# Two index conversions moved behind the last output projection's sums

## The chip, the cores and the metric

The kernel runs on one core of one Trainium2 chip. The metric is device time in microseconds (us) of one execution. An execution that was also recorded by the hardware profiler gives the trace; its times count from the first instruction, and the time from first to last instruction is the span.

## The reference, cut to what matters

One layer over 8 sequences of 1024 tokens with 512 features, all in float32:

```python
xn = _layernorm(x)
s = rnn(xn)                  # three projections 512 -> 1024 (W1), gates, a scan over time, then @ W2 (1024 -> 512)
f = (silu(xn @ sg) * (xn @ su)) @ sd          # shared feed-forward
f += routed(xn)              # each token to the one of 32 experts with the highest logit:
                             #   xs = xn * sigmoid(top logit);  (silu(xs @ gw[e]) * (xs @ uw[e])) @ dw[e]
x = x + s * silu(f)
```

## The kernel before, in words

The work has two stages with a short passage between them.

**Stage one** walks over 16 chunks of 512 tokens. For each chunk it computes the W1 projections, the scan and the shared feed-forward's hidden values, and projects the previous chunk's results out through W2 and the shared down matrix. All products of this stage use a seven-product scheme for 2x2 blocks, so operands are sums and differences of blocks. The order of all instructions is written out by hand: `at(slot, step)` puts a step into a numbered slot, a loop counts `now` up and runs the steps of each slot, and `due(now)` says how many matmuls of the output projection (`fill`, the generator `project_out`) must have been issued by then. Each engine carries out its instructions in the order in which they were issued.

One output projection is one `unit`: a chunk and a half (half 0 is W2, half 1 the shared down matrix). There are 32 units (n = 0 to 31). A unit has seven products of 16 matmul records each (8 matmuls of 128x128 by 128x256, each recorded twice), in the order `UNIT` = P1, P2, P6, P5, P7, P3, P4. P1, P6, P7 and P4 add up in one PSUM tile called `chain`; P2, P5 and P3 in one called `side`. The steps of a unit that matter here:

- L1007 (`out_combine`) makes the left operands: `s1` and `s3` on POOL (GpSimd), `s2` and `s4` on DVE (VectorE). P5 uses s1, P6 s2, P7 s3 and P3 s4.
- L1044 (ACT, ScalarE) copies P1's sum to SBUF (`a1`), later P6's (`a2`, same buffer) and P5's (`b5`).
- L1067 (DVE) adds P2's sum, read from `side`, and `a1` into the result tile `o[0]`. P5 starts `side` afresh, so it must come after L1067. L1067 itself writes a tile that the unit before has stored with L1028, so it must come after that store has landed.
- L1078 (DVE) adds P3's sum and `a2`; L1073 and L1081 (ACT) and L1074 (POOL) finish `o[1]`; L1028 (SP, SyncE) stores the results into `rec2`.
- L985 and L988 (`out_fetch`, SP) load a product's right operand, 512 KB, into a buffer of the pool `wo` or, for the last two units, `far`.

**The passage** builds the routing table. Each token gets a slot with its expert. The table has 186 columns of 128 rows. L1327 writes it to DRAM; L1330 (`ids`, DVE) makes an integer copy `idx`, by which whole rows are gathered: the first expert's inputs (L206, three gathers on POOL) and, later, what an expert needs at its end (L223). Experts 1 to 31 gather their inputs in quarter rows (L213), and need a second table, `fours`: index times 4 plus the quarter's number. `numbers(half)` makes one half of it. It issues four loads of the DRAM table from POOL (L1337) into a tile `number`, and puts one conversion (L1338, DVE, 128x372) into a later slot. Both halves are issued in one slot.

Around it stand, in the order of issue: the last unit (n = 31, half 1), the first expert's transposes on PE (L240) with their copies on DVE (L243), and the loads of the first expert's weights `e_wg`, `e_wu` and `e_wd` (L193, SP, 2 MB each). After it come four memsets of the experts' accumulators (L1489, DVE).

**Stage two** goes through 32 experts. For each, PE does eight rounds of gate, up and down products (L272, L261); ACT and DVE do the SiLU (L277, L279, L280); loads and gathers for the next two experts are issued between the rounds (L193, L213, L223), the next expert's inputs are transposed on DVE from round 5 on (L248), and results are scattered to the output (L360).

Of the kernel before, what the change touches and what calls it, by code (L numbers as in the profile page):

```python
# [33 lines left out]
def tile_kernel(  # L34
# [45 lines left out]
    nc = tc.nc  # L80
# [344 lines left out]
    now = 0  # L425
    steps = {}

    def at(slot, what, *args):
        assert slot >= now
        steps.setdefault(slot, []).append(lambda: what(*args))  # L430
# [655 lines left out]
    class Dispatch:  # L1086
# [245 lines left out]
        def numbers(self, half):  # L1332

            f = self.big([P, 2, NCOL], f"number{half}")
            rows = self.table.rearrange("(b c) q -> c b q", c=BL)[:, 2 * half : 2 * half + 2, :]
            for a in range(NA):
                nc.gpsimd.dma_start(out=f[a * BL : (a + 1) * BL, :, :], in_=rows)  # L1337
            at(now + 3, lambda: nc.vector.tensor_scalar(  # L1338
                pools["fours"][:, 2 * half : 2 * half + 2, :], f, float(NA), piece[:, 0:1],
                ALU.mult, ALU.add,  # L1340
            ))
# [247 lines left out]
```

## Time and profile before

| | |
|---|---|
| median of 3 runs | 4239.5 us (4238.96 to 4239.67) |
| the profiled execution: time | 4237.99 us |
| the profiled execution: span | 4236.3 us |
| PE (TensorE) busy | 4198.9 us, 99% of the span |
| DVE busy | 2083.9 us, 49% |
| ACT busy | 1978.0 us, 47% |
| POOL busy | 1105.3 us, 26% |
| granted TensorE clock, mean over the span | 0.997 of full speed |
| DMA | 925.61 MB, mean 218 GB/s |

PEld is PE's weight load, which runs beside its matmuls. In a timeline, each line gives the start, the duration, the engine and line of the kernel, the operation with output <- inputs and a count; the brackets give how long the engine stood idle ahead of it and what ended that. Entries with "q" (SPq, POOLq) are the engine's own queue of instructions, such as the issue of a transfer. "issue" as a releaser means that the profile shows no event that ended the wait. A transfer's landing is read from the completion events of its semaphore: every one of the 16 DMA engines reports its part.

### The profile page before, as it was taken

The page shows a single profiled execution, that of the slowest core. Times are in us where ns is not written, and L with a number is a line of the kernel's source. Part 1 is how long each engine was busy: PE and PEld are TensorE (multiplying, and loading weights), DVE is VectorE, ACT ScalarE, POOL GpSimd, SP SyncE. Part 2 cuts the span into 40 slices and gives each one's busy share as a digit, 9 for nine tenths or more (in the row PEclk, how much of TensorE's full clock was granted, in tenths as well). Part 3 has the DMA queues.
Part 4 walks back from the last instruction along what each step waited for, and adds up shares of the span by engine and source line. Part 5 has one row for each costly group of instructions (what it writes and reads, how often), then busy time and mean ns, then how long its engine had stood idle before and what let it go on. Part 6 is the DMA issues. An engine that isn't in the chain of part 4 may idle for free.

```text
span 4236.3 us, 51931 instructions
## 1 busy us (share of the span) xinstructions
PE 4198.9 (99%) x18719; PEld 3527.2 (83%) x18719; DVE 2083.9 (49%) x3425; ACT 1978.0 (47%) x3577; POOL 1105.3 (26%) x1182
## 2 busy tenths in 40 slices
PE   9999999999999999999999999999999999999998
PEld 4688888888888888888888888866777788889998
DVE  5555555544554545555545456424444444544444
ACT  5676676666666766666767666501111111111110
POOL 3222122111221121212211225442232333323221
PEclk9999999999999999999999999999999999999999
DMA  8767666666676666766666656575666567677773
GB/s 277 244 214 231 207 216 216 210 223 206 213 226 216 217 213 203 231 202 216 222 210 220 214 177 205 179 267 181 211 227 226 205 236 242 222 253 242 243 263 113
DMA packets 506854, 925.61 MB, mean 218 GB/s; under 512 B 38397, under 2 KB 324509, under 8 KB 498402
## 3 DMA queue, kind: packets, MB, share of 16 engines
q1 hardware_dynamic: 478754, 831.89, 59.2%
q0 software_dynamic: 27840, 90.36, 6.4%
q8 instruction: 150, 2.46, 0.2%
q14 instruction: 110, 0.90, 0.1%
HBM read 805.27 MB, written 134.92 MB: 222 GB/s over the span
## 4 chain that ended last, share of the span: by engine, by line
PE 97%; DVE 1%; DMA 1%; issue 0%; ACT 0%; POOL 0%; SPq 0%; POOLq 0%; ACTq 0%
PE b L759 24%; PE u L1055 18%; PE c L759 12%; PE e_u L272 11%; PE e_g L272 11%; PE acc L261 11%; PE a L759 6%; PE b L710 3%; PE lgp L520 0%; DMA e_xs<-rec,idx 0%; PE lgt L530 0%; PE b L725 0%; DMA x<-in_L_attn_x_dram 0%; DMA e_rest<-rec,idx 0%; POOL s L1007 0%
## 5 line engine op out<-in xcount | busy, mean ns | idle before, releaser
L759 PE MATMUL b<-t,sums 128*128 128x256 f32 x2400 | 616.1, 379 | 1.2 <-DVE t L681 1.2
L1055 PE MATMUL u<-wP,s 128*128 128x256 f32 x2032 | 598.4, 380 | 6.1 <-issue 6.1
L277 ACT ACTIVATE e_sig<-e_g 128x280 f32<-128x280 f32 (+15 forms) x256 | 101.8, 398 | 931.8 <-PE e_g L272 931.6
L272 PE MATMUL e_u<-e_xsT,e_wu 128*128 128x296 f32 (+15 forms) x2048 | 518.0, 396 | 0.0
L272 PE MATMUL e_g<-e_xsT,e_wg 128*128 128x296 f32 (+15 forms) x2048 | 518.0, 396 | 0.0
L261 PE MATMUL acc<-e_h,e_wd 128*128 128x296 f32 (+15 forms) x2048 | 512.8, 396 | 0.0
L759 PEld LDWEIGHTS b<-t,sums 128*128 128x128 f32 x2400 | 454.8, 190 | 63.0 <-ACT a L773 1.3
L272 PEld LDWEIGHTS e_g<-e_xsT,e_wg 128*128 128x128 f32 x2048 | 389.1, 190 | 87.2
L272 PEld LDWEIGHTS e_u<-e_xsT,e_wu 128*128 128x128 f32 x2048 | 389.1, 190 | 87.1
L261 PEld LDWEIGHTS acc<-e_h,e_wd 128*128 128x128 f32 x2048 | 389.1, 190 | 87.1
L1055 PEld LDWEIGHTS u<-wP,s 128*128 128x128 f32 x2032 | 387.2, 191 | 61.1 <-issue 8.3
L279 DVE TENSOR_TENSOR e_sig<-e_sig,e_g 128x280 f32<-128x280 f32 (+15 forms) x256 | 113.1, 442 | 481.6 <-ACT e_sig L277 481.2
L213 POOL DMA_INDIRECT e_xs<-rec,fours x276 | 262.4, 951 | 178.2 <-DMA e_rest<-rec,idx 86.0
L759 PE MATMUL c<-xnT,sums 128*128 128x256 f32 x1200 | 308.0, 379 | 0.0
L759 PE MATMUL c<-t,sums 128*128 128x256 f32 x1200 | 308.0, 379 | 0.0
L759 PE MATMUL b<-xnT,nat 128*128 128x256 f32 x1200 | 308.0, 379 | 0.0
L759 PE MATMUL a<-xnT,nat 128*128 128x256 f32 x1200 | 308.0, 379 | 0.0
L759 PE MATMUL b<-t,nat 128*128 128x256 f32 x1200 | 308.0, 379 | 0.0
L360 POOL DMA_INDIRECT out_dram<-e_rest,idx x84 | 93.1, 1109 | 801.2 <-DVE e_rest L359 798.2
L759 PEld LDWEIGHTS b<-xnT,nat 128*128 128x128 f32 x1200 | 228.0, 190 | 31.4 <-issue 0.5
L759 PEld LDWEIGHTS a<-xnT,nat 128*128 128x128 f32 x1200 | 228.0, 190 | 31.0
L759 PEld LDWEIGHTS c<-t,sums 128*128 128x128 f32 x1200 | 228.0, 190 | 31.0
(243 smaller groups left out, 6381.2 us busy)
## 6 DMA issues: line engine op xcount, KB each, us to landing
sums<-sdram SPq DMA_DIRECT2D x300, 512.0 KB, 4.6
nat<-in_L_attn_W_dram SPq DMA_DIRECT2D x192, 512.0 KB, 4.6
e_wg<-L_ffn_routed_gate_w_dram SPq DMA_DIRECT2D x32, 2048.0 KB, 8.4
e_wu<-n_L_ffn_routed_up_w_dram SPq DMA_DIRECT2D x32, 2048.0 KB, 12.7
e_wd<-L_ffn_routed_down_w_dram SPq DMA_DIRECT2D x32, 2048.0 KB, 19.0
wP<-tdram SPq DMA_DIRECT2D x127, 512.0 KB, 3.5
nat<-L_ffn_shared_gate_w_dram SPq DMA_DIRECT2D x64, 512.0 KB, 4.9
nat<-n_L_ffn_shared_up_w_dram SPq DMA_DIRECT2D x64, 512.0 KB, 4.3
```

The source lines that it names most:

```text
L213: nc.gpsimd.indirect_dma_start(out=r[:, b, :], out_offset=None, in_=rec1.rearrange("n (a d) -> (n a) d", a=NA), in_offset=bass.IndirectOff ...
L261: nc.tensor.matmul(accs[m][:, :W], lhsT=wd[:, j, m * P : (m + 1) * P], rhs=h[:, :W], start=(j == 0), stop=(j == NI - 1),)
L272: nc.tensor.matmul(o[:, :W], lhsT=w[:, k, j * P : (j + 1) * P], rhs=xsT[:, k, :W], start=(k == 0), stop=(k == KH - 1),)
L277: nc.scalar.activation(sig[:, :W], g[:, :W], AF.Sigmoid)
L279: nc.vector.tensor_tensor(sig[:, :W], sig[:, :W], g[:, :W], ALU.mult)
L360: store = nc.gpsimd.indirect_dma_start(out=of[:, :], out_offset=bass.IndirectOffsetOnAxis(ap=col[:n, :], axis=0), in_=o, in_offset=None, b ...
L710: nc.tensor.matmul(ps[:, part], lhsT=natural[n][:, k, block * P : (block + 1) * P], rhs=xnTs[0][:, k, part], start=(k == 0), stop=(k == KH ...
L759: nc.tensor.matmul(ps, lhsT=lhs[:, k, :], rhs=rhs[:, k, :], start=(new and k == 0), stop=(k == KQ - 1),  skip_group_check=True,)
L1055: nc.tensor.matmul(ps[:, q, :], lhsT=lhs[:, q * P : (q + 1) * P], rhs=w[:, p, :],  start=(q == 0 and p == 0 and name in ("P1", "P2", "P5") ...
```

## The change

The slot of the two conversions moves from 3 behind the issue of their loads to 26 behind. Nothing else is edited.

```diff
             for a in range(NA):
                 nc.gpsimd.dma_start(out=f[a * BL : (a + 1) * BL, :, :], in_=rows)
-            at(now + 3, lambda: nc.vector.tensor_scalar(
+            at(now + 26, lambda: nc.vector.tensor_scalar(
                 pools["fours"][:, 2 * half : 2 * half + 2, :], f, float(NA), piece[:, 0:1],
                 ALU.mult, ALU.add,
             ))
```

In the built program only DVE's order differs; the other four engines have the same instructions in the same order. On DVE, from the last part of s2 on:

| before | after |
|---|---|
| L1007 s2, last two parts | L1007 s2, last two parts |
| **L1338 fours, two conversions** | L1007 s4, four parts |
| L1007 s4, four parts | L1067 (after P2) |
| L1067 (after P2) | L243, three copies |
| L243, three copies | L1078 (after P3) |
| L1078 (after P3) | **L1338 fours, two conversions** |
| L1489, four memsets | L1489, four memsets |

## The prediction

> **What bounds the kernel now.** I read the page first, then the chain of work that ended last, then the passage between the stages engine by engine.
>
> ```profile
> PE 4198.9 (99%) x18719; PEld 3527.2 (83%) x18719; DVE 2083.9 (49%) x3425; ACT 1978.0 (47%) x3577; POOL 1105.3 (26%) x1182
> PE 97%; DVE 1%; DMA 1%; issue 0%; ACT 0%; POOL 0%; SPq 0%; POOLq 0%; ACTq 0%
> ```
>
> PE is the bound, and a change on DVE can matter only where PE stands still for it. PE's busy time leaves 4236.3 - 4198.9 = 37.4 us of the span, part of it at the two ends. In the chain in order of time, cut to the passage, one hole shows:
>
> ```profile
> 2763.51 5.81 issue
> 2769.33 5.83 PE u L1055 x16
> 2775.16 1.43 PE e_tp L240 x12
> 2776.59 10.37 PE u L1055 x48
> 2786.96 2.53 PE e_g L272 x8
> ```
>
> PE does nothing from 2763.27 (the end of P6's last record) to 2769.33, 6.06 us. Then P5 of the last unit runs (the x16), the transposes, P7, P3 and P4 (the x48), and the first expert. What held P5 is told by DVE's timeline and the waits of 2750 to 2770:
>
> ```profile
> 2753.93 1.27 DVE L1007 TENSOR_TENSOR s<-s,sh 128x256 f32<-128x256 f32 x2 [3.33 <-POOL s L1007]
> 2762.33 1.40 DVE L1338 TENSOR_SCALAR fours<-number,piece 128x372 int32<-128x372 f32 x1 [7.12 <-DMA number<-table]
> 2766.87 0.41 DVE L1338 TENSOR_SCALAR fours<-number,piece 128x372 int32<-128x372 f32 x1 [3.15 <-DMA number<-table]
> 2767.20 1.42 DVE L1007 TENSOR_TENSOR s<-sh,s 128x256 f32<-128x256 f32 x4
> 2768.54 0.68 DVE L1067 TENSOR_TENSOR o<-u,a 128x512 f32<-128x512 f32 x1
> ```
> ```profile
> ACT a L1044 <- DVE o L1067: 12.3, 1, 12.3
> DVE fours L1338 <- DMA number<-table: 10.3, 2, 7.1
> ```
>
> DVE stands 10.3 us in front of the conversions, whose loads land last at 2766.75. Behind them wait s4 and L1067, and behind L1067 P5, because it starts the PSUM tile that L1067 reads. L1067 ends at 2769.22, P5's weight load begins at 2769.30. P5's other inputs were there long before: its weights landed at 2761.30, s1 was made by 2754.6.
>
> The hole costs more than its length. By windows, PE's granted clock:
>
> ```profile
> 2760.00:2763.27 3.27, 3.27 (x16) 2.53 (x14) 0.94 (x1) 0.00 (x0) 3.06 (x5) 1.00 1.07 364
> 2763.27:2769.33 6.06, 0.00 (x1) 0.03 (x1) 2.81 (x7) 0.02 (x1) 0.23 (x1) 0.79 1.04 422
> 2769.33:2772.00 2.67, 2.67 (x6) 2.13 (x7) 0.00 (x0) 0.57 (x1) 0.00 (x0) 0.50 1.00 356
> 2772.00:2775.00 3.00, 3.00 (x12) 2.48 (x11) 0.00 (x0) 0.00 (x0) 0.00 (x0) 0.72 1.03 389
> 2775.00:2778.00 3.00, 3.00 (x21) 2.82 (x20) 1.85 (x3) 0.58 (x1) 0.00 (x0) 1.00 0.96 357
> ```
>
> The third number from the right is the clock. It is 1.00 before the hole, 0.50 behind it, 1.00 again from 2775; the trace's clock record has half speed from 2766.83 to 2773.66. So from P5's start to the transposes' first record (2774.99 in the timeline) 5.66 us went by, where 16 records take 3.45 us at full clock (10.37 / 48 = 0.216 each): 2.21 us lost.
>
> **The change part by part.** No work is added or removed. Two conversions and their wait move on DVE, past s4, L1067, three copies and L1078; no DMA and no other queue's instruction moves.
>
> *Part one: what was queued behind the conversions.* s4's four parts can run when s2 is done, at 2755.2. L1067 needs P2's sum (done at about 2759.8), a1 (copied by 2757.0) and its target tile. That tile is still being stored: the unit before issued its store at 2750.63, and the last completion came at 2762.99. That is the next late thing. L1067 then starts 0.12 us later (so long as the second conversion started after its landing, 2766.87 - 2766.75), takes 0.68, and PE follows 0.11 us behind it (2769.33 - 2769.22). P5 starts at 2762.99 + 0.12 + 0.68 + 0.11 = 2763.90 instead of 2769.33.
>
> *Part two: PE from there, at full clock.* A stop of 0.6 us should leave the clock alone: the kernel's only mid-span stop that cost clock was of 6.06 us, half speed coming 3.56 us into it. P5 ends at 2763.90 + 3.45 = 2767.35, the transposes at 2768.78 (their gathers landed at 2759.91), P7 at 2772.23 (its weights landed at 2764.43, s3 was done at 2763.51).
>
> *Part three: the wait that takes its place.* P3's right operand is a late load. SP's queue in the passage:
>
> ```profile
> 2753.60 0.37 SPq L1028 DMA_DIRECT2D rec<-o  x1
> 2754.16 0.36 SPq L193 DMA_DIRECT2D e_wu<-n_L_ffn_routed_up_w_dram  x1
> 2756.39 0.39 SPq L985 DMA_DIRECT2D far<-L_ffn_shared_down_w_dram  x1
> 2759.85 0.33 SPq L988 DMA_DIRECT2D far<-tdram  x1
> 2760.37 0.72 SPq L193 DMA_DIRECT2D e_wd<-L_ffn_routed_down_w_dram  x1
> ```
>
> The DMA engines are full from 2746 to 2778 (share 0.96 to 1.07 in each window, 321 to 422 GB/s), and these transfers land in the order of issue: the store at 2765.83, e_wu's 2 MB at 2771.22, the first far (P3's) at 2772.70, the second far (P4's) at 2773.98, e_wd at 2780.25. Nothing ahead of them in any queue moves, so I keep these times. P3 can then start at 2772.70 + 0.12 = 2772.82, 0.59 us after P7's end; P4's operand is there when P3 ends. P3 and P4 are 32 x 0.216 = 6.91 us: the first expert starts at 2779.73. In the records it started at 2786.79. **Sum: -7.06 us**, that is 5.43 (P5's start) + 2.21 (the clock) - 0.59 (P3's new wait), to 0.01.
>
> *Part four: the conversions in their new place.* Both halves have landed by 2766.75, so they wait for nothing but L1078, which ends at about 2776.3 + 0.2 + 0.7 = 2777.2. The first took 1.40 us while POOL ran s3 beside it, the second 0.41; both bounds give 0.8 to 2.8 us, and as POOL is then idle I take 0.8. They end at 2778.0 (at most 2780.0). Behind them stand the memsets (2.0 us), which the first down product needs only at 2796.90 - 7.06 = 2789.8: cover of 7.8 to 9.8 us. POOL's first gather for expert 1, issued at 2782.22 in the trace, can go at 2778.1; against PE's work it is 7.06 - 4.1 = 3 us later. The cover: expert 1's inputs are first transposed at 2827.9, 7 us earlier after the change, so at 2820.8. Its 11 gathers at 1.25 us end at about 2792 on POOL; in the trace the eleventh landed at 2802.2, so the slack of 26 us becomes 23. Cost zero.
>
> *The rest.* From 2786.96 on the chain is PE without a hole up to the last expert, so the whole sum arrives at the end. The profiled execution would go from 4237.99 to 4230.9; off the median of 4239.5, which lies 1.5 us above it, **4232.4 us** (-0.17%). I give the second.
>
> [...] Row: half speed began 3.56 us into the hole and ended 4.33 us after P5's start. [...]
>
> **The rivals.**
>
> *A larger gain.* [...] Chance 0.22, most of it on the far side of 0.2%.
>
> *A smaller gain.* [...] Chance 0.12.
>
> *The change doesn't do what it says:* P5 is held by something else that also ended at 2769.2. Against it: L1067's end and P5's weight load are 0.08 us apart, and no transfer that P5 needs lands near. 4239.5. Chance 0.04.
>
> *Slower.* The gathers of expert 1 now wait on POOL for the conversions, which wait for P3. Should they come so late that the inputs land behind 2820.8, DVE's transpose would hold the SiLU queued behind it, and PE with it. That decides from 23 us of delay on; the price is the delay beyond it, and the first 7 us of that only eat the gain. A delay of 40 us, as if the gathers waited out the 8 MB of weights that follow (2788 to 2824 in the trace), gives 4232.4 + 17 = 4249. Chance 0.04.
>
> **How the numbers follow.** Forecast 4232.4 with 0.58 (its own range 4231.4 to 4233.6). 0.2% is 8.5 us, about what a measurement of this kernel can tell from no change, so the bound is at 4231.0: my forecast is a gain that falls short of it. Faster by more: most of the larger gain, with what lies beyond it, 0.20. Slower by more: 0.04. Within: 0.76. The range from 4230.5 to 4234.8 takes in forecast, larger and smaller gain.
>
> **What would show it.** Right: in the profile after, DVE goes from s2 to s4 without a stop; L1067 starts at about 2763.1; PE's hole of 6.06 us becomes two of about 0.6, in front of P5 and P3; the clock stays 1.00; the first expert starts near 2779.7; the conversions run near 2777 at 0.4 us each. Wrong: another hole in front of P5, P7 or P4, a stretch of half clock, gathers of expert 1 that hold L248, or a PE that waits again later and gives the 7 us back.

## The result and the profile after

The changed kernel takes **4231.99 us** (median of 19 runs, 4230.77 to 4234.32), the kernel before 4239.84 us (19 runs, 4238.96 to 4240.6). The ratio is **0.9982**, its 95% interval 0.9975 to 0.9989: a gain of 7.85 us. That is a little less than the 8.5 us (0.2%) that the prediction set as its bound, though the interval reaches beyond it. The forecast was 4232.4.

The profiled execution of the changed kernel took 4234.32 us (span 4232.6), the longest of its 19 runs, as that of before (4237.99) was below the shortest of its own. So the two traces differ by 3.7 us where the medians differ by 7.85, and their spans don't measure the gain. What they do measure is **the passage**: from the first record of P1 of the last unit to the first product of the first expert. It lasted 34.05 us before (2752.74 to 2786.79) and 28.09 us after (2753.43 to 2781.52). No instruction outside the passage is moved. The rest of the time was 4237.99 - 34.05 = 4203.94 us before and 4206.23 after. In four more profiled executions, of the runs below on two chips like the first, it was 4204.70, 4204.94, 4205.33 and 4206.46. So it varies by 2.5 us from execution to execution. Therefore I compare passages between traces, and medians between times.

The page's first line, to be held against that of before: PE's busy time is 1.1 us less, and its idle time 34.8 us instead of 37.4. Of the busy time, P5 alone takes 2.14 us less (3.69 instead of 5.83); elsewhere PE is busy 1.0 us longer.

```profile
PE 4197.8 (99%) x18719; PEld 3525.8 (83%) x18719; DVE 2082.8 (49%) x3425; ACT 1979.9 (47%) x3577; POOL 1105.4 (26%) x1182
```

PE's timeline through the passage:

```profile
2753.43 7.07 PE L1055 MATMUL u<-far,sh 128*128 128x256 f32 x32
2760.78 3.69 PE L1055 MATMUL u<-wP,s 128*128 128x256 f32 x16 [0.28 <-DMA wP<-tdram]
2766.10 3.69 PE L1055 MATMUL u<-wP,s 128*128 128x256 f32 x16 [1.63 <-POOL s L1007]
2769.63 1.59 PE L240 MATMUL e_tp<-ident,e_xs 128*128 128x128 f32 x12
2771.07 3.63 PE L1055 MATMUL u<-wP,s 128*128 128x256 f32 x16
2774.54 3.69 PE L1055 MATMUL u<-far,s 128*128 128x256 f32 x16
2778.07 3.62 PE L1055 MATMUL u<-far,sh 128*128 128x256 f32 x16
2781.52 2.69 PE L272 MATMUL e_g<-e_xsT,e_wg 128*128 128x376 f32 x8
```

P6, P5, the transposes, P7, P3, P4 and the first expert follow each other; the hole of 6.06 us ahead of P5 has become 1.63. The bracket names POOL's s3 as what ended it, but P5 doesn't read s3 (P7 does): it is only the event that came last. DVE's timeline has the true one:

```profile
2755.81 1.42 DVE L1007 TENSOR_TENSOR s<-sh,s 128x256 f32<-128x256 f32 x4
2765.31 0.69 DVE L1067 TENSOR_TENSOR o<-u,a 128x512 f32<-128x512 f32 x1 [8.08 <-DMA rec<-o]
2770.30 1.85 DVE L243 COPY e_xsT<-e_tp 128x512 f32<-128x512 f32 x3 [4.30 <-PE e_tp L240]
2778.34 0.69 DVE L1078 TENSOR_TENSOR o<-u,a 128x512 f32<-128x512 f32 x1 [6.18 <-PE u L1055]
2778.95 0.73 DVE L1338 TENSOR_SCALAR fours<-number,piece 128x372 int32<-128x372 f32 x2
```

s4 follows s2 at once. L1067 waits 8.08 us for the store of the unit before, ends at 2766.00, and P5 starts 0.10 us later. The conversions run behind L1078 without a wait, 0.73 us for both. The third number from the right is the clock again, in two of the stretches that stood at 0.79 and 0.50 before:

```profile
2763.27:2769.33 6.06, 4.43 (x21) 3.61 (x20) 0.69 (x1) 0.59 (x1) 2.03 (x4) 1.00 1.07 427
2769.33:2772.00 2.67, 2.67 (x20) 2.52 (x19) 1.70 (x3) 0.59 (x1) 0.00 (x0) 1.00 0.94 368
```

By the trace's clock record it is 1.00 throughout the passage. So the conversions, P5's hole and the half clock are linked as the prediction had it; the sizes of the waits that remain have to be settled.

### The profile page after: what moved, and what is told of

Its sections match the earlier page's. It is cut to its first block, busy times and chain, and to the rows that moved or that the text cites. A ratio compares the mean times of both kernels' runs of the same rounds, so it can differ in the third digit from the quotient of the medians.

```text
span 4232.6 us, 51931 instructions
## 1 busy us (share of the span) xinstructions
PE 4197.8 (99%) x18719; PEld 3525.8 (83%) x18719; DVE 2082.8 (49%) x3425; ACT 1979.9 (47%) x3577; POOL 1105.4 (26%) x1182
## 4 chain that ended last, share of the span: by engine, by line
PE 97%; DVE 1%; DMA 1%; issue 0%; ACT 0%; POOL 0%; SPq 0%; POOLq 0%; ACTq 0%
PE b L759 24%; PE u L1055 18%; PE c L759 12%; PE e_u L272 11%; PE e_g L272 11%; PE acc L261 11%; PE a L759 6%; PE b L710 3%; PE lgp L520 0%; DMA e_xs<-rec,idx 0%; PE lgt L530 0%; PE b L725 0%; DMA x<-in_L_attn_x_dram 0%; DMA e_rest<-rec,idx 0%; DMA out_dram<-e_rest,idx 0%
## 5 line engine op out<-in xcount | busy, mean ns | idle before, releaser
L759 PEld LDWEIGHTS b<-t,nat 128*128 128x128 f32 x1200 | 228.0, 190 | 31.0
```

Of the source, the lines that this page charges most:

```text
L759: nc.tensor.matmul(ps, lhsT=lhs[:, k, :], rhs=rhs[:, k, :], start=(new and k == 0), stop=(k == KQ - 1),  skip_group_check=True,)
```

## The experiments

**Theory 1**, that of the prediction: P5 waited for L1067, L1067 in DVE's order for two conversions whose loads came late, and the hole brought half clock; what remains are two waits on a full DMA queue (DMA share 0.94 to 1.07 in the windows from 2760 to 2778), L1067's for the store and P3's for its operand (the first load into `far`). Its rivals: the loads in the queue make the passage long whatever DVE's order is, or P5 is held by something else. Kernels that are compared in time ran on one chip, with runs of the kernel before on the same. The passage is split at P5's start, so that the first part shows what held P5 and the second the clock and P3's wait.

| kernel | P1 to P5 | P5 to first expert | passage | time against before, same chip |
|---|---|---|---|---|
| before | 16.59 | 17.46 | 34.05 | |
| forecast for the change | 11.16 | 15.83 | 26.99 | |
| changed | 12.67 | 15.42 | 28.09 | 0.9982 [0.9975, 0.9989] |
| changed, second trace | 11.33 | 16.61 | 27.94 | 0.9981 [0.9972, 0.999] |
| changed, third trace | 11.85 | 16.83 | 28.68 | 0.9983 [0.9974, 0.9992] |
| changed, fourth trace (stage two's loads later, 7) | 10.72 | 16.78 | 27.50 | 0.9983 [0.9974, 0.9992] |
| 1, conversions behind s4, ahead of L1067 | 15.81 | 17.57 | 33.38 | 0.9996 [0.9987, 1.0005] |
| 2, conversions behind L1067 | 11.47 | 16.16 | 27.63 | 0.9988 [0.9979, 0.9997] |
| 3, PE kept busy in the hole | 15.86 | 15.33 | 31.19 | 0.9992 [0.9983, 1.0001] |
| 4, changed, first expert's weights later | 10.36 | 15.25 | 25.61 | 0.9974 [0.9964, 0.9985] |
| 5, before, first expert's weights later | 19.33 | 18.26 | 37.59 | 1.0008 [0.9999, 1.0017] |
| 6, changed, own tile for L1067 | 10.36 | 17.23 | 27.59 | 0.998 [0.9971, 0.9989] |

Runs 1 to 4 were on a second chip, and 5, 6 and the second trace of the changed kernel on a third. There every kernel takes some 14 us more than on the first (the kernel before 4255.15 and 4253.95 us), by a hole in stage two that is shown further below. The third and fourth trace come from a chip without it. Ratios are taken on each chip. The hole is not of one length, so on the second and third chip the passages say more than the times.

**1 and 2. Which of the operations behind the conversions matters.** Only the slot differs from the kernel before: 10 puts the conversions behind s4, 12 (in place of the 10 of the diff) behind L1067 too.

```diff
-            at(now + 3, lambda: nc.vector.tensor_scalar(
+            at(now + 10, lambda: nc.vector.tensor_scalar(
```

> Conversions behind s4 but still ahead of L1067 (slot 10). First theory (P5 is held by L1067, and L1067 by the conversions' loads, which land at 2766.75): L1067 follows the second conversion at 2767.3, P5 starts at 2768.1, 1.3 us sooner than before, and the half clock stays: 4239.8 - 1.3 = 4238.5 us, give or take 0.7. Rival (what the change freed was s4, P3's operand): s4 runs at 2755.8 as in the changed kernel, so the time is that of the changed kernel, 4232.0.

> Conversions directly behind L1067, ahead of the three copies and of L1078 (slot 12). First theory: only the place ahead of or behind L1067 counts; conversions end at about 2768 and the copies need DVE from 2769 on, so 4232.0 us as in the changed kernel, give or take 0.7. Rival (the conversions must stand behind all sums of the last unit): the copies or L1078 are held and the time lies over 4234.

Measured: 4251.65 and 4248.93 us, the kernel before 4255.15. PE's timeline of the first, at P5:

```profile
2767.93 5.93 PE L1055 MATMUL u<-wP,s 128*128 128x256 f32 x16 [5.29 <-issue]
```

The hole of 5.29 us and the half clock stay (16 records in 5.93 us instead of 3.69) as long as L1067 stands behind the conversions; taking s4 out from behind them changes the passage by 0.67 us, no more than the passages of the changed kernel differ among themselves. The second kernel puts them behind L1067. Its P5 and P3, and L1067:

```profile
2764.33 3.69 PE L1055 MATMUL u<-wP,s 128*128 128x256 f32 x16 [0.95 <-POOL s L1007]
...
2773.51 3.69 PE L1055 MATMUL u<-far,s 128*128 128x256 f32 x16 [0.59 <-DMA far<-L_ffn_shared_down_w_dram]
```
```profile
2763.53 0.69 DVE L1067 TENSOR_TENSOR o<-u,a 128x512 f32<-128x512 f32 x1 [6.88 <-DMA rec<-o]
```

Here stand the two waits of the prediction, 0.95 ahead of P5 (predicted 0.63: 2763.90 - 2763.27) and 0.59 ahead of P3. The prediction's 0.59 for P3 counts from where the next record could follow P7; counted so, it is 0.77 here (2773.51 - 2769.29 - 3.45). So in the passage the position behind L1067 is what counts; the other 14 slots of the change are not needed for it. In the time the picture is less sharp: this kernel gained 6.2 us by the medians and some 5 by the ratio, on a chip where the runs of the kernel before spread over 7 us (4250.91 to 4257.99). In its trace the hole in stage two is also 3.2 us longer than in the changed kernel's second trace (section 7), though that was taken on another chip.

**3. The clock by itself.** The kernel before, with ten more matmuls between P6 and P5, whose result nothing reads:

```diff
+        def filler(ps, rhs): [nc.tensor.matmul(ps[:, :HC], lhsT=ident, rhs=rhs, start=True, stop=True) for _ in range(10)]
...
-                w = out_w.pop((u, name))
+                w = (n == 31 and name == "P5" and filler(ps_w.tile([P, 512], FP, tag="w", name="junk"), w[:, 0, :])) or out_w.pop((u, name))
```

> The kernel before, with ten matmuls of no use (4.3 us, their result is read by nothing) on PE between P6 and P5 of the last unit, in the hole in which PE waits. P5's start stays, the clock should not fall. First theory (2.2 to 3.4 us of the gain is half clock behind the hole): 4239.8 - 2.2 to 4239.8 - 3.4, that is 4236.4 to 4237.6 us, granted clock 1.00 through the passage. Rival (the clock has no part, the whole gain is PE's waiting): 4239.8, give or take 0.5.

Measured: 4251.76 us, 3.4 below before, though work was added; the interval of the ratio just reaches 1. P5 still waits (the first two lines), and the clock stays at 1.00 where it fell before (the last two, by windows):

```profile
2762.82 4.48 PE L1031 MATMUL junk<-wP,ident 128*128 128x256 f32 x20
2768.32 3.69 PE L1055 MATMUL u<-wP,s 128*128 128x256 f32 x16 [1.02 <-issue]
```
```profile
2766.00:2769.00 3.00, 1.98 (x10) 1.45 (x9) 2.22 (x6) 0.59 (x1) 0.00 (x0) 1.00 0.98 418
2769.00:2772.00 3.00, 3.00 (x16) 2.64 (x16) 0.00 (x0) 0.00 (x0) 0.00 (x0) 1.00 1.03 374
```

What the filler removed in the passage is the half clock: the second part of the passage fell from 17.46 to 15.33 us. The half clock cost **2.13 us** (2.21 in the sum). The other 0.73 of the passage comes from loads that landed earlier in this execution (L1067 at 2767.53, 15.07 us behind P1, instead of 15.80).

**4 and 5. The DMA queue.** The first expert's weights, which stand ahead of the store and P3's load in SP's queue or between them, are issued 10, 10 and 1 steps later, in the changed kernel (4) and in the kernel before (5):

```diff
-    chunks[0].weight("g")
...
-        if k in (10, 20):
-            chunks[0].weight("ud"[k // 20])
+        if k in (10, 20, 21):
+            chunks[0].weight("gud"[(10, 20, 21).index(k)])
```

> The changed kernel, with the first expert's weights issued later on SP: e_wg behind the stores of unit 30, e_wu and e_wd behind the last operand of unit 31. First theory (what is left in the passage is the full DMA queue: L1067 waits for a store, P3 for its operand, both behind the weights): both land 4 to 5 us sooner, PE has no hole ahead of P5 and P3, and 1.4 to 2.5 us more go: 4229.5 to 4230.6 us. Rival (the weights are then the late thing, or the waits come from elsewhere): PE waits for e_wu at the first expert, 4232 or more.

> The kernel before, with the first expert's weights issued later as in the fourth experiment (g at step 10, u at 20, d at 21 of the loop). Theory 1 (in the kernel before, P5 stands behind the conversions, and these wait for their loads in a DMA queue that is full): the loads landed at about 2768.6 in the fourth experiment, so the conversions still end late, P5 starts at 2769 to 2771, a hole of 6 to 10 us with half clock behind it remains, the passage (P1 of the last unit to the first expert) is 33 to 37 us, and the time lies within 3 us of the kernel before, on either side. Rival (it is the weights in the queue that make the passage long, whatever DVE's order): the passage falls to 25.6 to 30 us, as in the fourth experiment, and the time by 4 to 8 us.

Measured: 4243.81 us (4), the kernel before 4255.15; 4257.24 us (5), the kernel before 4253.95 on that chip. The fourth kernel's PE has no hole left in the passage:

```profile
2752.11 7.07 PE L1055 MATMUL u<-far,sh 128*128 128x256 f32 x32
2759.01 7.07 PE L1055 MATMUL u<-wP,s 128*128 128x256 f32 x32
```

P6 and P5 now run as one group of 32, and the passage is 25.61 us, PE's own work. P3's operand has landed at 2769.90, 0.91 us before P3 starts. So the two waits of the changed kernel both come from where the weights stand in the queue. In the kernel before, the same order makes the passage 3.5 us longer:

```profile
2773.14 6.62 PE L1055 MATMUL u<-wP,s 128*128 128x256 f32 x16 [8.80 <-issue]
```

The conversions' loads are not helped by it (the second conversion started at 2770.68 instead of 2766.87), so the hole is 8.80 us. All this is somewhat more than theory 1 allowed: P5 at 2773.14 instead of 2769 to 2771, a passage of 37.59 instead of at most 37, a time 3.29 us up instead of at most 3. It refutes the rival all the same: with DVE's order as before, a better order of the transfers gains nothing. It costs 3.5 us in the passage; of the time that is not shown, since the interval reaches 1. One hides the other: the reordering of the queue pays only once the conversions are out of L1067's way.

**6. Are the two waits worth their sum?** The changed kernel, with the last unit's `o[0]` in a tile that no store has to leave first:

```diff
+            if n == 31: o[0] = hp.tile([P, 2, H], FP, tag="r", name="o_own", bufs=5)
```

> The changed kernel, with the last unit's result o[0] in a tile of its own name, so that L1067 no longer waits for the store of the unit before to land. Theory 1 (two waits in series behind the same DMA queue: behind the store comes P3's far load, issued 5 us after it): L1067 runs as soon as P2's sum is done, near 2760, P5 follows P6 with no hole, but P3 then waits for the far load, which lands at 2772.7 to 2774.4. The first expert starts at 2779.7 to 2781.4 whatever P5 did, so the time is within 1.0 us of the changed kernel's, at most 0.6 us better. Rival (the store's landing is the bound that is left): the first expert starts 1.0 to 1.7 us sooner, and the time falls by that.

> The changed kernel once more, for comparison on the same chip. Theory 1: 0.9980 to 0.9985 of the kernel before (6.2 to 8.5 us less), the passage 27.5 to 28.5 us with the clock at 1.00, where the kernel before has 33.5 to 34.5 us. [...]

> The fourth experiment's kernel once more, beside the changed kernel on the same chip. Theory 1: the two waits that the change left (the store ahead of L1067, the far load ahead of P3) go, the passage is 25.6 us, 2.0 to 2.6 us shorter than the changed kernel's, and the time is 2 to 2.6 us below it, about 0.9978 of the kernel before. Rival (the later weights make the first expert wait, or stage two's loads come later and give the gain back): the passage is as short, but the time is not below the changed kernel's.

Measured, for the sixth kernel, the changed one (its second trace) and the fourth: 4245.27, 4245.91 and 4243.19 us; the kernel before 4253.95. PE's timeline of the sixth, and P3 in the changed kernel:

```profile
2758.18 7.07 PE L1055 MATMUL u<-wP,s 128*128 128x256 f32 x32
...
2771.88 3.69 PE L1055 MATMUL u<-far,s 128*128 128x256 f32 x16 [1.74 <-DMA far<-L_ffn_shared_down_w_dram]
```
```profile
2774.51 3.69 PE L1055 MATMUL u<-far,s 128*128 128x256 f32 x16 [1.05 <-DMA far<-L_ffn_shared_down_w_dram]
```

P5 starts with P6, but P3 waits 1.74 us instead of 1.05. Of the 0.97 us gained ahead of P5 (11.33 - 10.36), 0.62 are given back behind it (17.23 - 16.61), and the time is 0.64 us lower, with ranges that overlap. The last completion of P3's operand came at 2771.74 here and at 2774.38 in the changed kernel's trace; P3 starts 0.13 to 0.14 us behind it in both. Counted from P1, that makes P3 0.35 us earlier here, and this is the whole difference of the two passages. It lies within what the changed kernel's own traces differ by, so no gain of the tile is shown. The waits are in series behind one queue: what is taken from the first comes back in the second. Of the changes tried here, only the queue's order takes away both: the fourth kernel is 2.72 us below the changed one, for a passage 2.33 us shorter.

**7. Stage two, and the best version.** On the second and third chip PE stands still in stage two as well. The changed kernel, first on the third chip and then on the first, by windows:

```profile
2798.00:2804.00 6.00, 6.00 (x21) 3.61 (x20) 0.00 (x0) 0.00 (x0) 4.47 (x6) 1.00 1.04 368
2804.00:2817.00 13.00, 6.63 (x11) 2.33 (x10) 1.55 (x3) 0.86 (x2) 5.22 (x6) 0.69 1.01 368
```
```profile
2798.00:2804.00 6.00, 6.00 (x21) 3.61 (x20) 0.55 (x1) 0.00 (x0) 4.48 (x6) 1.00 1.04 367
2804.00:2817.00 13.00, 13.00 (x43) 7.84 (x42) 2.18 (x4) 0.97 (x2) 5.20 (x6) 1.00 1.02 370
```

On the third chip PE is busy for 6.63 of 13 us, and ACT has stood since 2789.8:

```profile
ACT e_sig L277 <- remote: 25.0, 1, 25.0
```

The DMA engines are as full on the one chip as on the other (1.01 and 1.02), and "remote" names nothing that the trace has. All eight traces of the two chips have this hole, whatever the passage looks like. It can be sized by the time from the first expert's first product to the second expert's: 60.64 us in each of the six traces of the other chips, 71.63 to 75.64 us here. So it costs 11.0 to 15.0 us and differs by 4 us between traces (72.57, 75.00, 74.95 and 72.67 in runs 1 to 4, 75.64 in run 5, 72.17 in run 6, 71.79 and 71.63 in the changed and the fourth kernel on the third chip). The kernel before was not traced on these chips, so how much of a time difference there is the hole's is not known; the passages don't contain it. To see whether full DMA engines are a condition, I put the stage-two loads of expert 1 at rounds 1, 3 and 5 of expert 0, each behind a small store of that round's SiLU result, and expert 2's first load at round 6, in the fourth kernel and in the changed one:

```diff
-                last = (j, h)
+                last = (j, h); self.h = h
...
+    gate = dram.tile([P, C], FP, name="gate")
...
-                    between[j].append(lambda tag=tag: chunks[1].weight(tag))
+                    between[1 + 2 * j] += [lambda: nc.sync.dma_start(out=gate[0:1, 0:64], in_=chunks[0].h[0:1, 0:64]), lambda tag=tag: chunks[1].weight(tag)]
...
-                between[3 if e == 0 else 1].append(lambda: chunks[e + 2].weight("g"))
+                between[6 if e == 0 else 1].append(lambda: chunks[e + 2].weight("g"))
```

> The fourth experiment's kernel, with the loads of expert 1's three weights and expert 2's first put 1, 2, 3 and 3 rounds of expert 0 later, each of expert 1's behind a small store of that round's SiLU result to DRAM, so that they can't be issued early. It is about the hole of 10 to 12 us that the runs of this chip have in stage two, at 2800 to 2815, and those of the first chip have not, while the DMA engines are full in both. Theory A (in the full DMA engines something that ACT and PE need, such as their instructions, comes late): with the engines not full between 2785 and 2815 the hole goes, and the time falls by 10 to 14 us below the fourth experiment's. Theory B (the hole is not from these transfers): it stays as long, and the time is within 2 us of the fourth experiment's. If the chip is one without the hole, the time is within 2 us either way and nothing is told apart.

> The changed kernel with the same later loads of stage two, the passage left as the change has it. Theory A: 10 to 14 us below the changed kernel, about 2.3 us above the kernel of the run before this one, since what the passage keeps (the store ahead of L1067, the far load ahead of P3) is not touched by stage two. Theory B: within 2 us of the changed kernel.

> The changed kernel once more, beside the two of this call. Any theory: 0.9980 to 0.9985 of the kernel before.

> The run with the stage-two loads spread, once more, since the chip of the last call had no hole in stage two. On a chip that has it (the kernel before at 4250 us or more): theory A, 18 to 25 us below the kernel before, 0.9945 to 0.9955 of it; theory B, 10 to 12 us below it, 0.9972 to 0.9977. On a chip without it: 8 to 9 us below, 0.9980, and the cause stays open.

Measured: 4230.82, 4232.83 and 4232.57 us, the kernel before 4239.3; and 4230.62 for the first again on another chip, the kernel before 4240.21 (ratio 0.9978 [0.9969, 0.9987]). Both chips turned out to be without the hole, so nothing is told apart, and **the cause of the hole stays open**. The spread loads are worth nothing on such a chip (4232.83 against 4232.57). In the first of them, the later weights of the fourth kernel gain 1.75 us over the changed kernel: ratio 0.998 [0.9971, 0.9989] to the kernel before, and the passage 25.62 and 25.61 us. The fourth kernel, with or without the spread loads, is the best version found (ratios 0.9974 to 0.998, whose intervals overlap that of the change).

## Why the prediction was right, point by point

*What held P5.* Right. P5 follows L1067's end by 0.10 us after the change as by 0.11 before; runs 1 and 2 show that it is the place before or behind L1067 that decides. The rival that something else held it is refuted.

*P5's start (5.43 us).* Right in kind, inexact in size. The forecast had P5 11.16 us behind P1; the four traces have 12.67, 11.33, 11.85 and 10.72. The term is the landing of the store at 2762.99, taken unchanged from before. In the profiled execution after, the store was issued 0.69 us later and its last completion came at 2765.19, 13.87 us after its issue instead of 12.36. In the three others it took 12.53, 13.05 and 11.92 us. So a landing behind this full queue, carried over from one execution to another, was off by up to 1.5 us.

*The half clock (2.21 us).* Right, and measured by itself: 2.13 us by run 3. After the change, from P5's first record to the transposes' first record is 3.53 us, where it was 5.66. The 3.4 us that the expectation of run 3 has as its upper end were the author's estimate, and no run shows such a loss: half the stretch behind P5's start is 2.27 us in run 1 and 2.97 in run 5 (last section).

*P3's new wait (0.59 us).* Right in kind, and it alone sets the end of the passage. In all four traces P3's first record starts 0.13 us behind the last completion of its operand (after: 2774.41 and 2774.54), and the first expert 6.98 us behind that record. P3 waited about 0 us in the first trace, then 1.05, 1.27 and 1.22 us; ahead of P5 it was 1.63, 0.80, 1.01 and 0.20 us. So what P5 loses or gains no longer matters as long as P7 is through by then, as in the three later traces; in the first the two came within 0.02 us of each other. The fourth shows it best: P5 hardly waits, and P3 does.

```profile
2763.37 3.69 PE L1055 MATMUL u<-wP,s 128*128 128x256 f32 x16 [0.20 <-issue]
2773.17 3.69 PE L1055 MATMUL u<-far,s 128*128 128x256 f32 x16 [1.22 <-DMA far<-L_ffn_shared_down_w_dram]
```

The sum had P3 20.08 us behind P1 (2772.82 - 2752.74); the traces have it at 21.11, 20.96, 21.71 and 20.53. These 0.4 to 1.6 us are nearly the whole difference between the passage of the sum, 26.99 us, and the measured 27.50 to 28.68. The mechanisms of the sum stand; the size that was off is the landing of P3's operand, which was kept as it was before.

*Why the median still came out within 0.5 us.* By the passages, the change gained 5.4 to 6.5 us where the sum had 7.06; by medians 7.85, 8.04 and 6.73 us. So in the result some 2 us of the gain are not found in the passages, and they make up for what the sum had too much. The passage of before is known from one execution only, and that execution's time was below all 19 that it is compared with. Had other executions lost more in the passage, that would be consistent with the difference; but no further trace of the kernel before was taken, so it is not shown. That the forecast came within 0.5 us is in this part chance.

*The conversions' new place (cost 0).* Right. They took 0.73 us, with no wait, behind L1078. POOL's gathers of expert 1 started at 2779.63, 1.89 us ahead of the first expert instead of 4.57 (2786.79 - 2782.22), so 2.7 us later against PE, where 3 was predicted. Their reader, L248, first ran at 2822.61, 41.1 us behind the first expert, the predicted distance (2820.8 - 2779.7), directly behind the DVE operation ahead of it. The slower rival, gathers that hold the SiLU, didn't come near.

*Forecast and chances.* The gain is 0.18% (interval 0.11% to 0.25%). The prediction gave a gain short of 0.2% the larger chance, and that is what the medians show; the interval doesn't settle on which side of 0.2% it lies. The smaller and the larger gain, which the range of 4230.5 to 4234.8 takes in, were the author's estimates; no run shows how the half clock of the kernel before varies between executions, and by medians the gain was 7.85, 8.04 and 6.73 us on three chips. What the traces show is that the four passages were 0.5 to 1.7 us longer than the sum's 26.99 us.

## What to carry to other kernels

DVE ran its instructions in the order of issue in the traces of before and after, so the wait cost what was queued behind it, not what it did itself: two conversions of 1.40 and 0.41 us, with 10.3 us of waiting for their loads, held PE for 6.06 us through one unrelated sum. After taking such a wait away, list the next wait of each operation that it released, and ask whether they hang on the same queue. If they do, look at the last of them first: in run 6, 0.62 of the 0.97 us gained at the earlier one came back behind it, and in run 4 the queue's order removed both (passage 25.61 us). The order of two repairs matters when one is judged by itself: later weights alone made the passage 3.5 us longer, and on top of the change they made it 2.3 us shorter (1.75 to 2.72 us by the medians).

## What the runs showed of the hardware that was not expected

A stop of PE of 5.29 us cost about as much clock as one of 6.06 and less than one of 8.80. Half speed lasted 6.82 us in run 1 (by its windows), 6.83 in the trace before (by the clock record) and about 10.2 in run 5 (by its windows); it began 3.00, 3.56 and about 4.5 us into the hole. In the passage, waits of up to 1.74 us (run 6) cost no clock: it is 1.00 in each window from 2760 to 2800. In stage two on the third chip, where PE's waits in the changed kernel's trace were 1.22, 1.62, 1.63, 1.32 and 0.41 us with one or two matmul records between them, the mean clock from 2804 to 2817 is 0.69. The windows of run 1 show the half speed on both sides of P5's start at 2767.93:

```profile
2765.64:2767.93 2.29, 0.00 (x0) 0.03 (x1) 1.01 (x2) 0.01 (x1) 0.00 (x0) 0.50 1.00 422
2767.93:2772.46 4.53, 4.53 (x11) 3.63 (x12) 0.00 (x0) 0.57 (x1) 0.00 (x0) 0.50 0.99 374
```

What is lost, worked out as half of the stretch behind P5's start, is 4.53 / 2 = 2.27 us here (2.97 behind the hole of 8.80 us, where half speed lasted to 5.94 us after P5's start). The passages agree: from P5 to the first expert they took 17.57 us in run 1 and 18.26 in run 5, 2.24 and 2.93 us more than the 15.33 of run 3 at full clock. What sets the start and the length of the half speed, no run here tells.

And the hole in stage two: on two of the chips, ACT stands still for up to 25 us, and PE with it for part of that (6.4 of the 13 us above, in which the mean clock is 0.69), with no releaser in the trace, at a place where the others run through. It costs 11 to 15 us, more than the change gains, and its cause is open.
